# Down projection of the experts and output projection of the attention with the weights stationary, the sums of two batches turned back

## The chip, the core and the metric

The kernel runs on one core of one Trainium2 chip. The metric is the device time of one execution in microseconds, as the median of several runs. One execution is also taken with the hardware profiler; its rows are used below.

## The reference, cut to what matters

There are 16 batches of 100 tokens with 256 features (x), and for each batch 361 context rows of 256 features with a mask. All is float32. Four blocks follow each other, each added to x:

```python
x = x + xattn0(layernorm(x), ctx)       # 16 heads of 64; query i sees the keys j with j % 100 == i
x = x + experts(layernorm(x))           # 8 experts of 192, the best 2 of a token, and a shared one of 192
x = x + xattn1(layernorm(x), ctx, mask) # tanh scores over the context, two scalars per token
x = x + bitlinear_ffn(layernorm(x))     # 256 -> 1024 -> 256, quantised
```

The two products that the change touches are the last ones of the first two blocks:

```python
out = attention_sums.reshape(b, n_q, 1024) @ Wout + bout          # 1024 -> 256
out = sum over experts and shared of  (silu(x @ Wg) * (x @ Wu) * weight) @ Wd   # 9 * 192 = 1728 -> 256
```

## The kernel before

The program first counts the masks and ranks the batches by the number of context rows that count. If every batch fits a table of capacities (`CAPS`, 96 down to 32 rows), which the given inputs do, it takes the path `batches(True, "f")`, and in it `staggered`. The other path (`attend`, `experts`, `score`) is compiled and not run.

`staggered` treats the batches in 8 pairs g. In stage t it weaves three streams: `attention(t + 2)`, `middle(t + 1)` (the experts, `experts_pair`, and the preparation of the scores, `prepare_pair`) and `last(t)` (`score_few` for the two batches, and beside it the feed-forward of the batch before). `weave` runs the streams, which are generators, by turns: it always advances the one with the smallest quotient of steps done and declared steps; declared are 47, 33 and 26. The instructions are emitted in this order, and a scheduler in the framework then sets their order on each engine by its own estimate; on the chip each engine takes its instructions in that fixed order. A pair starts its attention in stage t = g - 2, so stage t = -2 has an attention alone, t = -1 has no scores, t = 6 has no attention, and t = 7 has only scores and feed-forward.

**Attention of a pair** (`attend_pair`). The normalised tokens of both batches are turned (`turned_pair`, tile `xT`, 128 features by 2 x 100 tokens), and GpSimd adds the bias `bout` to x (line 640). Queries are made 128 of the 1024 columns at a time with the weights stationary and the 200 tokens of both batches moving (line 664). `project` (line 650) makes keys and later values of one batch the same way, 361 context rows moving; VectorE multiplies them by the queries (`prT`), TensorE sums over a head into the bank `psim`, and the softmax (`p`) goes through DRAM (`dp`) to be spread over partitions as `pb`. Then, batch by batch, VectorE multiplies the values by `pb` (line 725) and adds up over keys into `accT`, 128 partitions by 4 by 100. At the end of each batch the output projection runs:

```python
po = bank(f"po_{g}_{i}")
for c in range(NH):                       # NH = 8
    nc.tensor.matmul(po[:S, :D], lhsT=accs[c // 4][:, c % 4, :], rhs=wout[:, c, :], ...)
nc.vector.tensor_tensor(xs[i], po[:S, :D], xs[i], ALU.add)
```

So the 100 tokens are stationary and the 256 columns of Wout move; the sum comes out with tokens on partitions and is added to x by VectorE.

**Experts of a pair** (`experts_pair`). The nine experts' 1728 inner columns are 14 chunks of 128. `gated` makes two chunks of gate and up (banks `pgT`, `puT`, line 810) with weights stationary and 200 tokens moving; ScalarE's tanh and VectorE make `hT` of them, `weighted` multiplies by the routing weights, which come back from DRAM (`dw`, `wb`), and `lowered` (line 838) adds the chunk's part of the down projection to the bank `pd` (100 tokens by 2 batches by 256), which a product of zeros has cleared (line 846). There too the tokens of one batch are stationary and the 256 columns of Wd move. At the end VectorE adds `pd` to x (line 874).

**Preparation and scores.** `prepare_pair` transposes the context (bank `pcn`, tile `cn`), picks the rows that count (`pcc`), and makes the projections `tpp` and `fpp`. `score_few` lets VectorE add them (`hf`, line 990), ScalarE take the tanh (line 997) and TensorE sum (`rho`, line 976).

**Feed-forward.** `feed_forward` works in bfloat16 on integers: tokens turned (`pxi`, `xiT`), two halves of gate and up (`pfg`, `pfu`), a quantised `hi`, its turn (`phi`, `hiT`), and the down product `pfd`.

Every float32 product shows as two rows in the profile, each with its own load of the stationary side (PEld); a float32 transpose shows as one.

## Time and profile before

| | |
|---|---|
| median of 3 runs | 1182.46 us (1181.66 to 1182.7) |
| profiled execution | 1183.23 us, its span 1181.5 us |
| granted TensorE clock, mean | 0.938 |
| pd rows (line 838) | 448, 109.1 us busy |
| po rows (line 738) | 256, 59.8 us busy |
| pgT and puT rows (line 810) | 448 and 448, 89.3 and 87.9 us busy |
| transposes pcn (line 905) | 96 |

A row of the profile gives a line, an engine, an operation and the tiles out<-in; a stationary side of 128 rows and 100 columns is written 128*100. PE is TensorE, PEld its weight loads, DVE VectorE, ACT ScalarE, POOL GpSimd, SP the engine that issues most transfers. The span runs from the first to the last instruction. Rows of TensorE overlap each other, so the time that one takes in a dense stretch is read from the starts and not from its duration.

### The profile page before, as it was taken

The numbers are of one execution on the slowest core, as the hardware profiler recorded it, in microseconds if no ns is written. First come the engines' busy times: TensorE is split into PE (matmuls) and PEld (weight loads), VectorE is DVE, ScalarE is ACT, GpSimd is POOL, SyncE is SP. The second block draws the span as 40 slices with busy tenths as digits, with TensorE's granted clock in tenths as the row PEclk, the third lists the DMA queues.
The fourth block names the chain that finished last, engine by engine and source line by source line (L and its number), as shares of the span: only waits on it lengthen the run. The fifth ranks groups of instructions, "written<-read, shape, count | busy, mean of one in ns | idle before, by whom it ended". The sixth has DMA issues, their size and how long they took to land.

```text
span 1181.5 us, 15014 instructions
## 1 busy us (share of the span) xinstructions
PE 1044.0 (88%) x5558; PEld 678.5 (57%) x5558; DVE 843.4 (71%) x1999; ACT 355.6 (30%) x509; POOL 130.1 (11%) x244
## 2 busy tenths in 40 slices
PE   4969989899888999899997999899999999889553
PEld 4536757465455655657555665566656675567432
DVE  2356476758877788777888668777787768787765
ACT  0001102523333334333334223243233323253431
POOL 3010011000320003200130001200031001100100
PEclk9979999999998999999989899999989999989755
DMA  7851033001401013010230104110140103110000
GB/s 233 211 126 52 28 93 83 22 21 29 92 20 35 15 41 80 20 35 15 57 84 0 43 7 95 45 31 20 31 89 4 40 7 82 29 29 18 4 4 11
DMA packets 52463, 58.59 MB, mean 50 GB/s; under 512 B 9129, under 2 KB 51101, under 8 KB 52381
## 3 DMA queue, kind: packets, MB, share of 16 engines
q1 hardware_dynamic: 51564, 54.39, 18.8%
q10 hardware_dynamic: 816, 3.15, 0.7%
q8 instruction: 46, 0.75, 0.3%
q14 instruction: 37, 0.30, 0.1%
HBM read 54.36 MB, written 3.17 MB: 49 GB/s over the span
## 4 chain that ended last, share of the span: by engine, by line
PE 77%; DVE 14%; ACT 4%; POOL 2%; issue 2%; DMA 1%; SPq 0%; ACTq 0%; DVEq 0%; POOLq 0%
PE pkT L650 27%; PE rho L976 9%; PE pd L838 8%; PE pgT L810 7%; PE puT L810 6%; DVE hf L990 4%; PE pqT L664 3%; PE po L738 3%; ACT hf L997 2%; PE psim L692 2%; PE pfd L1118 2%; PE pfg L1081 1%; PE pcc L917 1%; PE pfp L951 1%; PE phi L1110 1%
## 5 line engine op out<-in xcount | busy, mean ns | idle before, releaser
L650 PE MATMUL pkT<-cT_f,wkv 128*128 128x361 f32 x1024 | 371.4, 497 | 17.7 <-DVE pb L725 16.5
L990 DVE TENSOR_TENSOR hf<-tpp,fpp 128x800 f32<-128x800 f32 (+6 forms) x280 | 254.8, 935 | 29.1 <-PE rho L976 15.4
L650 PEld LDWEIGHTS pkT<-cT_f,wkv 128*128 128x128 f32 x1024 | 192.6, 200 | 139.5 <-issue 38.6
L997 ACT ACTIVATE hf<-hf 128x1600 f32<-128x1600 f32 (+5 forms) x140 | 204.6, 1461 | 218.3 <-DVE hf L990 186.4
L976 PE MATMUL rho<-hf,win 128*32 128x480 f32 (+7 forms) x1280 | 141.1, 477 | 36.1 <-ACT hf L997 35.6
L682 DVE TENSOR_TENSOR prT<-pkT,qT 128x300 f32<-128x300 f32 x128 | 59.8, 467 | 75.3 <-PE pkT L650 66.3
L838 PE MATMUL pd<-wd,hT 128*100 128x256 f32 x448 | 109.1, 384 | 0.0
L838 PEld LDWEIGHTS pd<-wd,hT 128*100 128x100 f32 x448 | 72.0, 166 | 38.7 <-issue 14.1
L810 PE MATMUL pgT<-xT_e,wg 128*128 128x200 f32 x448 | 89.3, 341 | 0.0
L725 DVE TENSOR_TENSOR pb<-pkT,pb 128x361 f32<-128x361 f32 x128 | 64.7, 527 | 33.8 <-PE pkT L650 26.6
L810 PE MATMUL puT<-xT_e,wu 128*128 128x200 f32 x448 | 87.9, 338 | 0.0
L976 PEld LDWEIGHTS rho<-hf,win 128*32 128x32 f32 x1280 | 31.8, 114 | 97.1 <-ACT hf L997 52.3
L810 PEld LDWEIGHTS pgT<-xT_e,wg 128*128 128x128 f32 x448 | 77.2, 189 | 15.0 <-issue 5.6
L810 PEld LDWEIGHTS puT<-xT_e,wu 128*128 128x128 f32 x448 | 76.1, 189 | 4.8 <-issue 3.1
L822 ACT ACTIVATE hT<-pgT 128x400 f32<-128x400 f32 (+1 forms) x64 | 29.4, 460 | 141.6 <-PE pgT L810 134.2
L823 DVE SCALAR_TENSOR_TENSOR hT<-hT,pgT 128x400 f32<-128x400 f32 (+1 forms) x64 | 32.9, 514 | 52.3 <-ACT hT L822 51.6
L738 PE MATMUL po<-wout,accT 128*100 128x256 f32 x256 | 59.8, 381 | 0.0
L664 PE MATMUL pqT<-xT_a,wq 128*128 128x200 f32 x256 | 53.0, 355 | 1.9 <-ACT xT_a L634 1.9
L664 PEld LDWEIGHTS pqT<-xT_a,wq 128*128 128x128 f32 x256 | 44.8, 199 | 14.4 <-issue 9.0
L894 POOL TENSOR_SCALAR at<-iota,place 128x96 f32<-128x96 f32 (+15 forms) x48 | 42.2, 898 | 85.8 <-PE pcc L917 83.6
L738 PEld LDWEIGHTS po<-wout,accT 128*100 128x100 f32 x256 | 42.1, 169 | 12.5 <-issue 0.9
L898 POOL TENSOR_SCALAR negf<-iota,cnts 128x96 f32<-128x96 f32 (+7 forms) x16 | 11.9, 741 | 336.4 <-DVE sf L1004 336.1
(221 smaller groups left out, 1127.0 us busy)
## 6 DMA issues: line engine op xcount, KB each, us to landing
pb<-dp SPq DMA_DIRECT2D x64, 361.0 KB
wb<-dw SPq DMA_DIRECT2D x32, 200.0 KB
cT_f<-in_ctxT_dram SPq DMA_DIRECT2D x16, 361.0 KB
wb<-dw SPq DMA_DIRECT2D x32, 100.0 KB
wkv<-in_L_xattn_Wkv_dram ACTq DMA_DIRECT2D x2, 1024.0 KB
x_f<-in_x_dram SPq DMA_DIRECT2D x16, 100.0 KB
out_dram<-x_f SPq DMA_DIRECT2D x16, 100.0 KB
dp<-p SPq DMA_DIRECT2D x8, 180.5 KB
```

The costliest lines, as they stand in the source:

```text
L650: nc.tensor.matmul(ps[:, :T], lhsT=wkv[:, k, at : at + P], rhs=cTs[i][:, k, :], start=k == 0, stop=k == NK - 1,)
L664: nc.tensor.matmul(ps[:, i * 2 * S : (i + 1) * 2 * S], lhsT=wq[:, k, (c + i) * P : (c + i + 1) * P], rhs=xT[:, k, :, :].rearrange("p b s - ...
L682: nc.vector.tensor_tensor(pr[:, :BACK].rearrange("p (c s) -> p c s", s=S), kp[:, :BACK].rearrange("p (c s) -> p c s", s=S), q.unsqueeze(1) ...
L725: nc.vector.tensor_tensor(pb[:, j, :], vp[:, :T], pb[:, j, :], ALU.mult)
L738: nc.tensor.matmul(po[:S, :D], lhsT=accs[c // 4][:, c % 4, :], rhs=wout[:, c, :], start=c == 0, stop=c == NH - 1,)
L810: nc.tensor.matmul(ps[: rows[c], c * 2 * S : (c + 1) * 2 * S], lhsT=w[:, k, (c0 + c) * P : (c0 + c) * P + rows[c]], rhs=xT[:, k, :, :].rea ...
L823: nc.vector.scalar_tensor_tensor(h_, h_, 1.0, pg_, ALU.add, ALU.mult)
L838: nc.tensor.matmul(pd[:, i, :], lhsT=h[: rows[c], at : at + S], rhs=wd[: rows[c], c0 + c, :], start=False, stop=c0 + c == NFC - 1 and i == 1,)
L894: nc.gpsimd.tensor_scalar(at[:rows, c, :], iota[:rows, :cap], place[:rows, c, b : b + 1], None, ALU.is_equal)
L976: nc.tensor.matmul(rho[32 * j : 32 * j + 32, : FM * cap], lhsT=win[:, k, 31 - r : 63 - r], rhs=h2[:, n * cap : (n + FM) * cap], start=r == ...
L990: nc.vector.tensor_tensor(h[:, f : f + n // 2, :], tp[:, k, :].unsqueeze(1).to_broadcast([P, n // 2, cap]), fp[:, k, r * nb + f : r * nb + ...
L997: nc.scalar.activation(h2, h2, AF.Tanh)
```

## The change

The two projections change sides. In `lowered`, 128 of the 256 columns of Wd are stationary and the 200 tokens of both batches move; `pd` holds 128 output features by two halves by 200. In `attend_pair` the same is done with Wout; for this the values of both batches are finished first (the loop over groups of four chunks is now outside, the one over batches inside), and one `po` of both batches comes at the end. A new function, `turned_back`, copies such a bank to SBUF with ScalarE (`dT`; for the attention with the bias added there, in two activations), and, one step later, lets TensorE transpose it in four pieces into a bank `pback`, which VectorE adds to x.

With the bias on partitions, `bout` is loaded as 128 by 2 single elements, GpSimd's adds go, and the path that is not run loads its own row. Room in SBUF is made by sharing: `p` takes a buffer of `prT`, `hiT` one of `hT2`, and `cn` holds one half of the features at a time, so that the picking of the first half precedes the transposes of the second. The declared steps become 45, 34 and 26, and the next pair is loaded at the attention's step 36 in place of 38. The streams have 47, 34 and 26 steps.

```diff
     wr, wr_src = weight("wr", ins["L0_ffn_W_gate_router"], E)
     wt, wt_src = weight("wt", ins["L1_xattn_Ws"], D)
     wf, wf_src = weight("wf", ins["L1_xattn_W"], D)
-    bout = const.tile([S, D], FP, tag="bout", name="bout")
+    bout = const.tile([P, NK], FP, tag="bout", name="bout")
     ebias = const.tile([S, E], FP, tag="ebias", name="ebias")
     wg = const.tile([P, NK, EF], FP, tag="wg", name="wg")
     wu = const.tile([P, NK, EF], FP, tag="wu", name="wu")
...
 
     def load_others():
         load = nc.sync.dma_start
-        load(out=bout, in_=ins["L0_xattn_bout"].to_broadcast([S, D]))
+        with nc.allow_non_contiguous_dma(reason="a few columns"):
+            load(out=bout, in_=ins["L0_xattn_bout"].rearrange("o (k p) -> p (o k)", p=P))
         load(out=ebias, in_=ins["L0_ffn_expert_bias"].to_broadcast([S, E]))
         load(out=wout, in_=wout_src)
         load(out=wr, in_=wr_src)
...
 
     def attend(b, x, cT):
         xn = layernorm(x, f"a{b}")
-        nc.gpsimd.tensor_tensor(x, x, bout, ALU.add)
+        brow = work.tile([S, D], FP, tag="brow", name=f"brow_{b}", bufs=1)
+        nc.sync.dma_start(out=brow, in_=ins["L0_xattn_bout"].to_broadcast([S, D]))
+        nc.gpsimd.tensor_tensor(x, x, brow, ALU.add)
         yield
         xT = transposed(xn, f"a{b}")
         yield
...
         nc.scalar.copy(xT.rearrange("p k b s -> p (k b s)"), ps[:, : NK * 2 * S])
         return xT
 
+    def turned_back(ps, name, bias=None):
+
+        dT = work.tile([P, NK, 2, S], FP, tag="dT", name=f"dT_{name}", bufs=1)
+        if bias is None:
+            nc.scalar.copy(dT.rearrange("p k b s -> p (k b s)"), ps[:, : NK * 2 * S])
+        else:
+            for k in range(NK):
+                nc.scalar.activation(
+                    dT[:, k, :, :].rearrange("p b s -> p (b s)"), ps[:, k * 2 * S : (k + 1) * 2 * S],
+                    AF.Identity, bias=bias[:, k : k + 1],
+                )
+        yield
+        back = bank(f"pback_{name}").rearrange("p (b d) -> p b d", b=2)
+        for i in range(2):
+            for k in range(NK):
+                nc.tensor.transpose(back[:S, i, k * P : (k + 1) * P], dT[:, k, i, :], ident)
+        return back[:S]
+
     def attend_pair(g, xs, cTs):
         xns = normal_pair(xs, f"a{g}")
-        for x in xs:
-            nc.gpsimd.tensor_tensor(x, x, bout, ALU.add)
         yield
         yield
         xT = turned_pair(xns, f"a{g}")
...
                         psim[32 * j : 32 * j + 32, :T], lhsT=heads[:, at : at + 32], rhs=pr,
                         start=i == 0 and c0 == 0, stop=i == 1 and c0 > 0,
                     )
-        p = work.tile([P, NC_, S], FP, tag="p", name=f"p_{g}", bufs=1)
+        p = work.tile([P, NC_, S], FP, tag="prT", name=f"p_{g}", bufs=4)
         p2 = p.rearrange("p c s -> p (c s)")
         nc.gpsimd.memset(p2[:, T:], NEG)
         nc.scalar.copy(p2[:, :T], psim[:, :T])
...
         rows = dp.rearrange("(j r) t -> r j t", r=32)
         for _ in range(4):
             yield
-        for i in range(2):
-            accs = []
-            for c0 in range(0, NH, 4):
+        accs = []
+        for c0 in range(0, NH, 4):
+            acc = work.tile([P, 4, 2, S], FP, tag="accT", name=f"accT_{g}_{c0}")
+            for i in range(2):
                 pb = work.tile([P, 4, T], FP, tag="pb", name=f"pb_{g}_{i}_{c0}", bufs=2)
                 for e in range(2):
                     row = 4 * i + 2 * (c0 // 4) + e
...
                     vp = project(i, c0 + j, 1)
                     nc.vector.tensor_tensor(pb[:, j, :], vp[:, :T], pb[:, j, :], ALU.mult)
                     yield
-                acc = work.tile([P, 4, S], FP, tag="accT", name=f"accT_{g}_{i}_{c0}")
-                nc.vector.tensor_tensor(acc, pb[:, :, :S], pb[:, :, S : 2 * S], ALU.add)
+                own = acc[:, :, i, :]
+                nc.vector.tensor_tensor(own, pb[:, :, :S], pb[:, :, S : 2 * S], ALU.add)
                 for c in range(2, NC_):
                     nc.vector.tensor_tensor(
-                        acc[:, :, : KEYS[c]], acc[:, :, : KEYS[c]],
+                        own[:, :, : KEYS[c]], own[:, :, : KEYS[c]],
                         pb[:, :, c * S : c * S + KEYS[c]], ALU.add,
                     )
-                accs.append(acc)
-            yield
-            po = bank(f"po_{g}_{i}")
+            accs.append(acc)
+        yield
+        yield
+        po = bank(f"po_{g}")
+        for o in range(NK):
             for c in range(NH):
                 nc.tensor.matmul(
-                    po[:S, :D], lhsT=accs[c // 4][:, c % 4, :], rhs=wout[:, c, :],
+                    po[:, o * 2 * S : (o + 1) * 2 * S], lhsT=wout[:, c, o * P : (o + 1) * P],
+                    rhs=accs[c // 4][:, c % 4, :, :].rearrange("p b s -> p (b s)"),
                     start=c == 0, stop=c == NH - 1,
                 )
-            nc.vector.tensor_tensor(xs[i], po[:S, :D], xs[i], ALU.add)
-            yield
+        back = yield from turned_back(po, f"a{g}", bout)
+        for i in range(2):
+            nc.vector.tensor_tensor(xs[i], back[:, i, :], xs[i], ALU.add)
+        yield
 
     def experts_pair(g, xs):
         xns = normal_pair(xs, f"e{g}")
...
 
         def lowered(c0, h, rows):
             for c in range(2):
-                for i in range(2):
-                    at = (2 * c + i) * S
+                for o in range(NK):
                     nc.tensor.matmul(
-                        pd[:, i, :], lhsT=h[: rows[c], at : at + S], rhs=wd[: rows[c], c0 + c, :],
-                        start=False, stop=c0 + c == NFC - 1 and i == 1,
-                    )
-
-        yield
-        pd = psum_rho.tile([S, 2, D], FP, tag="down", name=f"pd_{g}")
+                        pd[:, o * 2 * S : (o + 1) * 2 * S],
+                        lhsT=wd[: rows[c], c0 + c, o * P : (o + 1) * P],
+                        rhs=h[: rows[c], c * 2 * S : (c + 1) * 2 * S],
+                        start=False, stop=c0 + c == NFC - 1 and o == NK - 1,
+                    )
+
+        yield
+        pd = psum_rho.tile([P, NK * 2 * S], FP, tag="down", name=f"pd_{g}")
 
         nc.tensor.matmul(
-            pd.rearrange("p b d -> p (b d)"), lhsT=zero.to_broadcast([1, S]),
-            rhs=zero.to_broadcast([1, 2 * D]), start=True, stop=False,
+            pd, lhsT=zero.to_broadcast([1, P]), rhs=zero.to_broadcast([1, NK * 2 * S]),
+            start=True, stop=False,
         )
         hs = {}
         for c0 in range(0, NFC + 4, 2):
...
             if 0 <= c0 - 4 < NFC:
                 lowered(c0 - 4, *hs.pop(c0 - 4))
             yield
+        back = yield from turned_back(pd, f"e{g}")
         for i in range(2):
-            nc.vector.tensor_tensor(xs[i], pd[:, i, :], xs[i], ALU.add)
+            nc.vector.tensor_tensor(xs[i], back[:, i, :], xs[i], ALU.add)
         yield
 
 
...
             nc.gpsimd.tensor_scalar(neg, iota[:, :cap], cnts[:, b : b + 1], -1e30, ALU.is_ge, ALU.mult)
             negs.append(neg)
 
-            cn = work.tile([P, NK, len(TC), P], FP, tag="cn", name=f"cn_{b}", bufs=1)
-            for k in range(NK):
+            for k in range(NK):
+                cn = work.tile([P, len(TC), P], FP, tag="cn", name=f"cn_{b}_{k}", bufs=1)
                 ps = bank(f"pcn_{b}_{k}")
                 for c, rows in enumerate(TC):
                     nc.tensor.transpose(
...
                     )
                 whole = T // P
                 nc.scalar.copy(
-                    cn[:, k, :whole, :].rearrange("p c d -> p (c d)"), ps[:, : whole * P]
-                )
-                nc.scalar.copy(cn[: TC[-1], k, whole, :], ps[: TC[-1], whole * P : (whole + 1) * P])
+                    cn[:, :whole, :].rearrange("p c d -> p (c d)"), ps[:, : whole * P]
+                )
+                nc.scalar.copy(cn[: TC[-1], whole, :], ps[: TC[-1], whole * P : (whole + 1) * P])
                 yield
-            for k in range(NK):
                 for c, rows in enumerate(TC):
                     to = (2 * k + i) * cap
                     nc.tensor.matmul(
-                        pcc[:, to : to + cap], lhsT=cn[:rows, k, c, :],
+                        pcc[:, to : to + cap], lhsT=cn[:rows, c, :],
                         rhs=at[:rows, c, :], start=c == 0, stop=c == len(TC) - 1,
                     )
             yield
...
             nc.tensor.transpose(
                 ps[:, c * S : (c + 1) * S], hi[:, c * P : (c + 1) * P], ident_bf[:S, :S]
             )
-        hiT = work.tile([P, HID // P, S], BF, tag="hiT", name=f"hiT_{b}", bufs=1)
+        hiT = work.tile([P, HID // P, S], BF, tag="hT2", name=f"hiT_{b}", bufs=4)
         nc.scalar.copy(hiT.rearrange("p c s -> p (c s)"), ps[:, : HID // P * S])
         yield
         ps = bank(f"pfd_{b}")
...
         def attention(g):
             xs, cTs, _ = zip(loaded.pop(2 * g), loaded.pop(2 * g + 1))
             for i, _ in enumerate(attend_pair(g, xs, cTs)):
-                if i == 38 and g + 1 < G:
+                if i == 36 and g + 1 < G:
                     load_pair(g + 1)
                 yield
             attended[g] = xs, cTs
...
         for t in range(-2, G):
             streams = []
             if t + 2 < G:
-                streams.append((47, attention(t + 2)))
+                streams.append((45, attention(t + 2)))
             if 0 <= t + 1 < G:
-                streams.append((33, middle(t + 1)))
+                streams.append((34, middle(t + 1)))
             if t >= 0:
                 streams.append((26, last(t)))
             if t == -1:
```

## The prediction

> **What bounds the kernel now.** I read the page first, then the busy time of the engines in the stretches between the starts of successive attention stages, then TensorE's timeline for the spacing of its rows, and last the three engines around one place where a stage ends and the next begins.
>
> The page: TensorE is busy 88% of the span and carries 77% of the chain that ended last; pkT, pd and po are among its largest lines.
>
> ```profile
> span 1181.5 us, 15014 instructions
> PE 1044.0 (88%) x5558; PEld 678.5 (57%) x5558; DVE 843.4 (71%) x1999; ACT 355.6 (30%) x509; POOL 130.1 (11%) x244
> PE 77%; DVE 14%; ACT 4%; POOL 2%; issue 2%; DMA 1%; SPq 0%; ACTq 0%; DVEq 0%; POOLq 0%
> ```
>
> By stage (columns: stretch, length, PE, PEld, DVE, ACT, POOL busy with counts, granted clock, DMA share, GB/s), a full stage has TensorE at 131.4 of 141 us and VectorE at 110.1. So a saving on TensorE counts, but only some 10 us of idle TensorE and 31 us of idle VectorE stand between the two limits. The last stretch, 87.5 us of the last pair's scores, has neither pd nor po and stays.
>
> ```profile
> 494.00:635.00 141.00, 131.37 (x698) 82.06 (x694) 110.11 (x251) 50.35 (x67) 17.53 (x28) 0.96 0.17 40
> 1094.00:1181.50 87.50, 43.42 (x324) 29.01 (x324) 57.16 (x156) 26.49 (x43) 4.99 (x13) 0.63 0.02 6
> ```
>
> TensorE's timeline (start, us, operation) shows what a row costs when rows stand back to back: take the difference of starts. pgT and puT are already 128 stationary columns with 200 moving; pd is 100 stationary with 256 moving.
>
> ```profile
> 1058.08 1.52 PE L810 MATMUL pgT<-xT_e,wg 128*128 128x200 f32 x8
> 1059.43 1.52 PE L810 MATMUL puT<-xT_e,wu 128*128 128x200 f32 x8
> 1060.79 0.50 PE L810 MATMUL pgT<-xT_e,wg 128*128 128x200 f32 x2
> 1061.13 1.89 PE L838 MATMUL pd<-wd,hT 128*100 128x256 f32 x8
> 1062.85 1.18 PE L810 MATMUL pgT<-xT_e,wg 128*128 128x200 f32 x6
> ```
>
> Eight pgT take 1059.43 - 1058.08 = 1.35 us, 169 ns each; eight pd take 1062.85 - 1061.13 = 1.72 us, 215 ns each.
>
> **The change, part by part.** The number of rows stays (448 for pd, 256 for po: two output halves in place of two batches), the moving side falls from 256 to 200 columns, so a row falls from 215 to 169 ns, 46 ns. pd: 448 x 46 = 20.6 us. po: 256 x 46 = 11.8 us. Both stand in full stages where TensorE is packed.
>
> The Trainium skill, page "TensorE: Matmul & The Clock Gate", section "LDWEIGHTS (loading the stationary operand)", speaks against this: a load takes its columns / 1.2 ns, whatever the rows. By that the 28 more columns cost 23 ns a row (an estimate from the page), 16 us in all if nothing hides them, and the change would end some 9 us slower. The trace has longer loads for the wider shape too (194 against 166 ns mean), but pgT with just that load is spaced at 169 ns, so the load is hidden, and I charge none of it.
>
> Added are 16 turns back of 4 transposes each, 64 rows of 128 moving columns. The nearest row is pcn, three transposes of 128x128 from 592.33 to 592.75, where rho starts: 0.42 / 3 = 140 ns. The lower end is pxT_f, four with 100 moving columns from 617.16 to 617.60, 110 ns. I take 140: 64 x 0.14 = 9.0 us (7.0 at the low end).
>
> The same page, section "Part 4: PE-mode transpose", gives about 275 ns for a transpose inside a kernel; by it the 64 would take 17.6 us (an estimate) and the change would come out 1.6 us slower than before. The trace's own 140 ns decides.
>
> TensorE work thus falls by 20.6 + 11.8 - 9.0 = 23.4 us, of which a full stage has 2.6 + 1.5 - 1.1 = 2.9 us.
>
> What it costs in waits. *The attention's turn* is the expensive one. Before, the first batch's po lay in mid-stage and only the second one's 16 rows ended the stage. Now all 32 rows stand at the end, the attention stream has 47 steps but is woven as 45, so its last steps run after the others have finished, and between po and the next stage come a ScalarE copy, four transposes and two adds. This is the same place before, TensorE, VectorE, ScalarE:
>
> ```profile
> 628.88 3.62 PE L738 MATMUL po<-wout,accT 128*100 128x256 f32 x16
> 632.34 0.34 PE L632 MATMUL pxT_a<-ident,xn_a 100*128 100x100 f32 x2
> 636.83 0.39 PE L632 MATMUL pxT_e<-ident,xn_e 100*128 100x100 f32 x2 [0.36 <-DVE xn_e L332]
> ```
>
> ```profile
> 629.54 3.36 DVE L990 TENSOR_TENSOR hf<-tpp,fpp 128x720 f32<-128x720 f32 x4 [0.45 <-ACT fpp L956]
> 632.83 0.41 DVE L742 TENSOR_TENSOR x_f<-po,x_f 100x256 f32<-100x256 f32 x1
> ```
>
> ```profile
> 629.08 0.74 ACT L956 ACTIVATE fpp<-pfp,cols 128x200 f32<-128x200 f32 x2 [1.89 <-PE pfp L951]
> 631.36 1.40 ACT L997 ACTIVATE hf<-hf 128x1440 f32<-128x1440 f32 x1 [1.53 <-DVE hf L990]
> 633.00 1.41 ACT L997 ACTIVATE hf<-hf 128x1440 f32<-128x1440 f32 x1 [0.23 <-DVE hf L990]
> ```
>
> After: 32 po rows of 169 ns from 628.88 end at 634.3. In the changed program's instruction order dT's two activations are queued on ScalarE behind both tanh (end 634.41); priced by fpp's pair they take 0.74, to 635.15. Transposes 0.56 and rho rows between them: VectorE's first add starts near 635.9, not 632.83. VectorE has finished its four hf at 632.9 and waits 3.0 us, with the next hf queued behind the add. Then two adds (0.41), two statistics (0.43), GpSimd's two steps (0.23 + 0.57) and xn_e (0.41) put the first pxT_e at about 639.2. TensorE has run out by 637.3 and waits 1.9 us; the rest of the queue (pqT, prt, rho) then brings pgT to about 646, 3.5 us after its old 642.49. Of these 3.5, the 16 po rows moved here (5.4 - 3.5 = 1.9) and the transposes (0.6) are in the sum already, so 1.0 us is new idle; VectorE had waits on GpSimd in that stretch of before and makes up the rest. Bounds 0 (rho and pqT cover it) and 3.0 (VectorE's stall passes through whole). I take 1.5, nearest to the 1.0 with some of VectorE's lateness left: 6 x 1.5. The first two boundaries have no scores to cover a turn: copy 0.74, transposes 0.56 and a second batch's normalisation behind them, 2.5 each. Sum 9.0 + 5.0 = 14.0 us.
>
> *The experts' turn*: the order puts six or more pkT rows, rho and the next stage's pieces between the last pd and the transposes, and a rho that needs a later tanh ahead of them; nothing waits on dT (0.49 us on ScalarE, by xT's row). Before, VectorE's add there waited for pd anyway (1.24 us at 581.1). Taken as 0, at most 0.5 each. The last pair's turn falls into 4.94 us in which TensorE waits for wbtf.
>
> *Ends of stages paced by VectorE*: phi waits 2.45 us for hi at 606.07. A TensorE that comes earlier waits longer where VectorE is dense. I charge 0.4 us for 6 stages, 2.4 us; the upper end is the whole 2.9 of a stage.
>
> *Answers of nothing*: 16 GpSimd adds of bout go (16 x 0.723 = 11.6 us of an engine busy 11%). bout's load in 4-byte pieces ranks with the cols loads on SP, issued in 0.37 to 0.47 us, and is first needed near 81 us. The SP order of dp, pb and context loads keeps its shape: the loads for the next pair still go just ahead of the last pb. cn, half as large, makes ScalarE's copy for k = 1 wait for pcc of k = 0, which now precedes pcn of k = 1 on TensorE. p in prT's buffers and hiT in hT2's take buffers whose readers are already past in TensorE's order; at worst a short wait on ScalarE, which is busy 30%.
>
> Sum: 23.4 - 14.0 - 2.4 = 7.0 us. Against the profiled execution, 1183.23 us (span 1181.5, 1.7 around it), 1176.2; the median of the runs, 1182.46, lies 0.8 lower, so 1175.5. About 0.2% (2.4 us) is what a measurement can tell from no change.
>
> **Rivals.** *The turns are covered* (0.20): rho, pxT_a and pqT fill the boundary, the 14.0 and 2.4 vanish: 1182.5 - 23.4 = 1159. For it: TensorE had gaps of only 0.3 us there. Against: the pxT_e order above.
>
> *VectorE keeps the pace* (0.10): each stage's 2.9 us return at phi and pwb: about 1182.
>
> *The boundary opens and the clock falls* (0.29, slower). After a stretch with TensorE half busy, the trace shows the granted clock near half:
>
> ```profile
> 646.00:652.00 6.00, 3.10 (x20) 0.57 (x16) 4.96 (x14) 3.98 (x3) 0.00 (x0) 0.81 0.00 0
> 652.00:657.00 5.00, 5.00 (x13) 2.91 (x12) 0.62 (x3) 0.54 (x2) 0.00 (x0) 0.55 0.15 47
> ```
>
> There eight pkT take 4.6 us (652.14 to 656.77) against 2.6 (584.23 to 586.86): 2.0 us. If VectorE's 3.0 us pass through and one such stretch follows, a boundary costs 5.0: 6 x 5.0 + 5.0 + 2.4 - 23.4 = +14.0, 1196.5. It decides from (23.4 - 2.4 - 5.0) / 6 = 2.7 us a boundary on. For it: 634 to 639 would hold some 2.6 us of TensorE work in 5. Against: TensorE before that is packed with po.
>
> **How the numbers follow.** Forecast 0.41 at 1175.5, own range 1168 to 1180; covered 0.20; paced 0.10; opened 0.29, from 1185 to 1200. Faster 0.41 + 0.20 = 0.61, same 0.10, slower 0.29. The range 1158 to 1195 leaves out under 0.1 on each side.
>
> **What would show it.** Right: pd and po rows at 169 ns, pback four in 0.56, VectorE idle about 3 us ahead of the pback adds, TensorE idle 1 to 2 us before pxT_e, experts' transposes without a wait. Wrong: po or pd spaced above 190 ns, a clock under 0.9 behind the boundary, or phi waiting over 4 us.

## The result and the profile after

The changed kernel takes **1200.4 us** (median of 4 runs, 1195.72 to 1202.33) against 1182.58 of the kernel before beside it (1181.66 to 1183.04). The ratio is 1.0146, 95% interval 1.0115 to 1.0176: 18 us slower, where 7 us less were forecast. The profiled execution took 1201.14 us with a span of 1199.3; before had 1181.5.

The page of the changed kernel, the lines that answer to those shown of before:

```profile
span 1199.3 us, 15155 instructions
PE 1051.0 (88%) x5622; PEld 714.2 (60%) x5622; DVE 842.4 (70%) x1999; ACT 363.2 (30%) x533; POOL 119.9 (10%) x228
PE 71%; DVE 16%; POOL 4%; ACT 4%; issue 2%; DMA 2%; SPq 0%; DVEq 0%; ACTq 0%; POOLq 0%
```

TensorE's busy time rose by 7 us although its rows became shorter, and it lost 6 points of the chain, of which VectorE and GpSimd took over 2 each (ScalarE stayed at 4%): the path now runs through them more often.

By stage (the same columns as before: length, busy times, granted clock): the stage that answers to 494 to 635, and the stretch from the start of the last eight pd rows to the end.

```profile
501.60:645.50 143.90, 131.61 (x701) 87.45 (x700) 109.01 (x249) 51.44 (x70) 17.09 (x26) 0.94 0.17 39
1101.70:1199.30 97.60, 52.38 (x337) 36.53 (x336) 59.99 (x163) 27.85 (x46) 5.00 (x13) 0.57 0.02 6
```

The stage is 2.9 us longer with TensorE as busy as before at a lower clock. The last stretch is 97.6 us at a clock of 0.57; counted from the same row, before has 90.2 at 0.64.

TensorE's timeline (start, us, operation) gives the new spacing:

```profile
1072.29 1.52 PE L835 MATMUL puT<-xT_e,wu 128*128 128x200 f32 x8
1073.98 1.52 PE L862 MATMUL pd<-hT,wd 128*128 128x200 f32 x8
1075.34 1.18 PE L835 MATMUL pgT<-xT_e,wg 128*128 128x200 f32 x6
```

Eight pd rows take 1075.34 - 1073.98 = 1.36 us, 170 ns each, as forecast; the wider load of the stationary side stays hidden. The section "LDWEIGHTS (loading the stationary operand)" of the Trainium skill's page "TensorE: Matmul & The Clock Gate" puts a load at its columns / 1.2 ns. For this shape that isn't a cost on top of the row: loads of 189 ns mean in the trace do not show in the spacing.

The boundary between two stages, on TensorE, VectorE and ScalarE:

```profile
768.40 7.02 PE L760 MATMUL po<-accT,wout 128*128 128x200 f32 x32
775.36 0.72 PE L1002 MATMUL rho<-hf,win 128*32 128x320 f32 x2
776.01 0.32 PE L655 MATMUL pback_a<-ident,dT_a 128*100 128x128 f32 x1
781.40 0.42 PE L635 MATMUL pxT_e<-ident,xn_e 100*128 100x100 f32 x2 [2.90 <-DVE mv_e L328]
```

```profile
769.11 3.03 DVE L1016 TENSOR_TENSOR hf<-tpp,fpp 128x640 f32<-128x640 f32 x4 [0.73 <-ACT fpp L982]
777.13 0.82 DVE L1016 TENSOR_TENSOR hf<-tpp,fpp 128x640 f32<-128x640 f32 x1 [4.99 <-PE rho L1002]
777.87 0.75 DVE L767 TENSOR_TENSOR x_f<-pback_a,x_f 100x256 f32<-100x256 f32 x2
```

```profile
772.23 1.27 ACT L1023 ACTIVATE hf<-hf 128x1280 f32<-128x1280 f32 x1 [0.20 <-DVE hf L1016]
775.46 0.75 ACT L647 ACTIVATE dT_a<-po,bout 128x200 f32<-128x200 f32 x2 [1.96 <-PE po L760]
```

VectorE makes two hf buffers in four instructions and then waits 4.99 us. It waits there not for the turned sums but for a buffer: `hpool` has two, the third hf needs the eight rho rows that free the first, and these stand on TensorE behind all 32 po rows, six of them also behind the first transpose (776.01), which waits for dT. ScalarE is done with both tanh at 773.5 and waits for po. Part of the po rows run at half clock (32 in 7.0 us, against 5.4 at 169 ns). Then come the turn, the adds, two statistics and GpSimd's steps, and TensorE waits 2.90 us for pxT_e. Over the whole kernel (view of waits: sum, times, longest):

```profile
PE pxT_e L635 <- DVE mv_e L328: 14.5, 7, 3.1
PE pxT_e L635 <- DVE xn_e L333: 5.5, 4, 2.9
DVE hf L1016 <- PE rho L1002: 33.3, 28, 5.0
```

Before, TensorE waited 3.8 us for pxT_e in all and VectorE 15.4 for rho.

### The profile page after: what moved, and what is told of

It is laid out like the page before. It is cut to its first block, busy times and chain, and to the rows that moved or that the text cites. A ratio compares the mean times of both kernels' runs of the same rounds, so it can differ in the third digit from the quotient of the medians.

```text
span 1199.3 us, 15155 instructions
## 1 busy us (share of the span) xinstructions
PE 1051.0 (88%) x5622; PEld 714.2 (60%) x5622; DVE 842.4 (70%) x1999; ACT 363.2 (30%) x533; POOL 119.9 (10%) x228
## 4 chain that ended last, share of the span: by engine, by line
PE 71%; DVE 16%; POOL 4%; ACT 4%; issue 2%; DMA 2%; SPq 0%; DVEq 0%; ACTq 0%; POOLq 0%
PE pkT L669 21%; PE rho L1002 8%; PE pgT L835 7%; PE puT L835 6%; PE pd L862 6%; PE pqT L683 5%; PE po L760 4%; DVE hf L1016 3%; PE psim L711 3%; ACT hf L1023 2%; PE pfd L1144 2%; PE pfp L977 2%; DVE pb L745 2%; DMA pb<-dp 2%; PE pfg L1107 1%
## 5 line engine op out<-in xcount | busy, mean ns | idle before, releaser
L669 PE MATMUL pkT<-cT_f,wkv 128*128 128x361 f32 x1024 | 362.5, 485 | 11.4 <-DVE pb L745 10.7
L669 PEld LDWEIGHTS pkT<-cT_f,wkv 128*128 128x128 f32 x1024 | 187.1, 195 | 122.3 <-issue 32.5
L1002 PE MATMUL rho<-hf,win 128*32 128x480 f32 (+7 forms) x1280 | 154.6, 476 | 32.5 <-ACT hf L1023 32.2
L862 PE MATMUL pd<-hT,wd 128*128 128x200 f32 x448 | 89.3, 337 | 0.0
L862 PEld LDWEIGHTS pd<-hT,wd 128*128 128x128 f32 x448 | 76.5, 189 | 18.8 <-issue 9.9
L683 PE MATMUL pqT<-xT_a,wq 128*128 128x200 f32 x256 | 64.6, 403 | 1.9 <-ACT xT_a L637 1.9
L683 PEld LDWEIGHTS pqT<-xT_a,wq 128*128 128x128 f32 x256 | 52.8, 230 | 9.5 <-issue 6.7
L760 PE MATMUL po<-accT,wout 128*128 128x200 f32 x256 | 50.9, 362 | 1.1 <-DVE accT L750 1.1
L760 PEld LDWEIGHTS po<-accT,wout 128*128 128x128 f32 x256 | 50.3, 214 | 1.7 <-DVE accT L750 1.4
L921 POOL TENSOR_SCALAR at<-iota,place 128x96 f32<-128x96 f32 (+15 forms) x48 | 36.2, 772 | 128.2 <-PE pcc L943 119.4
```

The lines of the kernel that those rows point to most:

```text
L669: nc.tensor.matmul(ps[:, :T], lhsT=wkv[:, k, at : at + P], rhs=cTs[i][:, k, :], start=k == 0, stop=k == NK - 1,)
L683: nc.tensor.matmul(ps[:, i * 2 * S : (i + 1) * 2 * S], lhsT=wq[:, k, (c + i) * P : (c + i + 1) * P], rhs=xT[:, k, :, :].rearrange("p b s - ...
L760: nc.tensor.matmul(po[:, o * 2 * S : (o + 1) * 2 * S], lhsT=wout[:, c, o * P : (o + 1) * P], rhs=accs[c // 4][:, c % 4, :, :].rearrange("p ...
L862: nc.tensor.matmul(pd[:, o * 2 * S : (o + 1) * 2 * S], lhsT=wd[: rows[c], c0 + c, o * P : (o + 1) * P], rhs=h[: rows[c], c * 2 * S : (c + ...
L921: nc.gpsimd.tensor_scalar(at[:rows, c, :], iota[:rows, :cap], place[:rows, c, b : b + 1], None, ALU.is_equal)
L1002: nc.tensor.matmul(rho[32 * j : 32 * j + 32, : FM * cap], lhsT=win[:, k, 31 - r : 63 - r], rhs=h2[:, n * cap : (n + FM) * cap], start=r == ...
```

## The experiments

The 25 us between forecast and result had candidates in every step, so the runs take the change apart. In all of them "the body" is the time up to the start of the last eight pd rows, and "the rest" what follows; both come from one profiled execution of each kernel, which can lie some us off the median. The executions of one kernel differ by their mean granted clock: no_turn took 1158.4 us at 0.935 and 1171.9 at 0.924, and its profile, 1158.9, is at 0.935. The table is the base of what follows.

| kernel | median us | ratio to before, 95% | body | rest |
|---|---|---|---|---|
| before | 1182.58 | | 1091.3 | 90.2 |
| after | 1200.40 | 1.0115 to 1.0176 | 1101.7 | 97.6 |
| cn_alone | 1185.37 | 1.0015 to 1.0043 | 1087.3 | 96.6 |
| experts_alone | 1197.20 | 1.0109 to 1.0182 | 1097.2 | 96.3 |
| attention_alone | 1203.94 | 1.0147 to 1.0220 | 1107.1 | 97.2 |
| cn_whole | 1189.40 | 1.0045 to 1.0095 | 1091.9 | 96.6 |
| no_turn | 1163.64 | 0.9806 to 0.9913 | 1061.3 | 95.8 |
| no_turn_att | 1166.95 | 0.9855 to 0.9903 | 1073.2 | 91.4 |
| no_turn_exp | 1179.36 | 0.9959 to 0.9991 | 1079.7 | 95.9 |
| copy_only | 1180.82 | 0.9973 to 1.0010 | 1083.9 | 95.5 |
| attention_whole | 1196.25 | 1.0102 to 1.0147 | 1102.1 | 90.0 |
| experts_sim | 1182.32 | 0.9974 to 1.0008 | 1085.1 | 96.2 |

**cn_alone**: the kernel before with the context's transpose halved as in the change, nothing else.

```diff
-cn = work.tile([P, NK, len(TC), P], FP, tag="cn", bufs=1)
 for k in range(NK):
+    cn = work.tile([P, len(TC), P], FP, tag="cn", bufs=1)
     ... transposes and copies of k ...
-for k in range(NK):
     ... pcc of k ...
```

> The kernel before with one part of the change alone: cn holds one half of the features at a time. Theory T (two causes): in the last pair's preparation nothing runs beside it, so transposes, ScalarE copies and picking of the halves go one after the other; in the changed kernel that stretch, from the start of the last pair-6 phi to the first rho of the last pair, is 23.2 us (1110.55 to 1133.73) against 16.2 (1099.69 to 1115.93). So 5 to 8 us slower here too, 1187 to 1191. Rival R (the turn and the granted clock make the whole loss, the stretch is longer only because the clock happened to be low there): within 2 us of before.

Measured +3.4 us, between the two. The body became shorter, the rest longer by 6.4 us.

**experts_alone**: the kernel before with the experts' projection and its turn as in the change.

```diff
-pd[:, i, :], lhsT=h[...], rhs=wd[: rows[c], c0 + c, :]
+pd[:, o * 2 * S : (o + 1) * 2 * S], lhsT=wd[..., o * P : (o + 1) * P], rhs=h[...]
+back = yield from turned_back(pd, f"e{g}")
```

> The kernel before with the experts' down projection alone changed: weights stationary, 200 tokens moving, its sum turned back, declared steps 34, hiT in hT2's buffers. Theory T: the saving of pd, 448 rows x 46 ns = 20.6 us less 32 transposes of 140 ns = 4.5 us, is mostly kept: 1166 to 1174. Rival R (a TensorE that is loaded less gets a lower clock, whatever is saved is lost): 1180 or more.

A miss: 1197.2, in the rival's range but not by its cause, for experts_sim below has as low a mean clock (0.929 against 0.930) and is 15 us faster. TensorE waits in front of pback_e, not for ScalarE's copy but for VectorE's pb (view of waits):

```profile
PE pback_e L652 <- DVE pb L743: 10.8, 6, 6.0
PE pback_e L652 <- ACT dT_e L641: 0.6, 1, 0.6
```

pb has nothing to do with the experts. What ties the two is the PSUM bank: `bank` hands out five in turn, and the one that the transposes get still holds a pkT that VectorE has not multiplied. Everything behind the transposes on TensorE waits too.

**attention_alone**: the change without its experts' part (halved cn stays).

```diff
-back = yield from turned_back(pd, f"e{g}")
-pd[:, o * 2 * S : (o + 1) * 2 * S], lhsT=wd[..., o * P : (o + 1) * P], rhs=h[...]
+pd[:, i, :], lhsT=h[...], rhs=wd[: rows[c], c0 + c, :]
```

> The changed kernel with the experts' down projection as before: the attention's part with its block of 32 po rows at the end of a stage, its turn, and the halved cn. Theory T: all of the loss is here, and the saving of pd is missing: above 1205. Rival R: between before and after, 1185 to 1200.

1203.9, between the two ranges, and as slow as the whole change. So neither part pays by itself, and they don't add up: experts_alone costs 15 us, attention_alone 22, both together 18.

**cn_whole**: the change with the whole cn kept; dT takes qT's buffers for want of space.

```diff
-dT = work.tile([P, NK, 2, S], FP, tag="dT", bufs=1)
+dT = work.tile([P, NK, 2, S], FP, tag="qT", bufs=3)
```

> The changed kernel with cn whole again (both halves of the features at once, dT in qT's buffers to make the room). Theory T: the last preparation is short again, 5 to 8 us off: 1192 to 1196. Rival R: as the changed kernel, 1198 to 1202.

1189.4, faster than the theory's range: the halved cn, which the prediction charged nothing for, costs 11 us here, 9.8 of them in the body. The theory's place for it, the last preparation, is wrong: from the last phi to the first rho of the last pair the changed kernel takes 23.2 us (1110.55 to 1133.73) and cn_whole still 22.4 (1100.73 to 1123.17). The same 5622 rows keep TensorE busy 1051.0 us in the changed kernel and 1043.8 here, and the mean granted clock is lower, 0.921 to 0.925 in its four executions against 0.927 to 0.930 in the five of cn_whole. Rows that the halving doesn't touch take longer: po 50.9 against 48.3 us, pfp 19.9 against 18.0, pqT 64.6 against 62.1, pkT 362.5 against 360.2. A clock lower by 0.007 over 1190 us is up to 8 us, so most of the cost seems to come by way of the clock; how the halving brings it down is not shown. dT's other buffers don't explain it: in both kernels dT waits for nothing but po and pd. By itself the halving cost the kernel before 3.4 us.

**before_again**: the kernel before, unchanged, to see whether the rest's 90.2 us are its own or one execution's.

> The kernel before, once more, for the granted clock of its last stretch. In the first profile the last 88 us have 64 us at half clock; in all four kernels tried so far that stretch is 95 us with 78 to 83 us at half clock, though cn_whole and experts_alone have the same instructions there. If the place of the clock's windows against the program decides (theory T), another execution of before shows 95 us too, with less half clock elsewhere, and 1182 all the same. If the changed kernels really differ there (rival R), it shows 88 us again.

1183.05, and a rest of 90.2 again, as the rival says: it goes with the program.

**no_turn**: cn_whole without the turns; VectorE adds po and pd as they lie.

```diff
-back = yield from turned_back(po, f"a{g}", bout)
+yield
-nc.vector.tensor_tensor(xs[i], back[:, i, :], xs[i], ALU.add)
+nc.vector.tensor_tensor(xs[i], po[:S, i * 100 : i * 100 + D], xs[i], ALU.add)
```

> cn_whole without the turns: no ScalarE copy, no transposes, VectorE adds parts of the banks pd and po to x as they are, so that the output projections' results are put in wrong places. Rows of 200 columns and the order of steps stay. Theory T (the turn at the stage's boundary takes back what the shorter rows bring): 704 x 46 ns = 32 us less, of which VectorE's pace may take a part: 1152 to 1168. Rival R (VectorE paces the stages, shorter rows bring nothing whatever the turn): 1175 or more.

1163.6, within the theory's range. In the body of these profiles the shorter rows bring 1091.3 - 1061.3 = 30.0 us; the two turns cost 1189.4 - 1163.6 = 25.8 us in the medians and 30.6 in the body.

**attention_first**: cn_whole with the attention declared as 54 steps for 45, so that po has other work beside it.

```diff
-streams.append((45, attention(t + 2)))
+streams.append((54, attention(t + 2)))
```

> cn_whole with the attention's declared steps 54 in place of 45: its last steps come at 47/54 of a stage, so the po block and the turn lie among the other streams' work. Theory T (the turn costs because nothing covers it): 5 to 15 us under cn_whole's 1189.4, unless the start of the next stage, which po covered before, opens instead. Rival R (the rows and the clock cost it, wherever the turn stands): 1187 to 1192.

A miss: 1199.96, worse by 10.6 us. The wait for pxT_e is gone, but po no longer fills the end of the stage, and TensorE waits there for the scores instead:

```profile
PE pwb L1057 <- ACT wbtf L1054: 34.4, 7, 5.2
```

In cn_whole that wait was 18.9 us. The mean granted clock fell too, from 0.930 to 0.916.

**po_split**: cn_whole with po in two halves of 16 rows, the first in mid-stage, in psim's bank.

```diff
-po = bank(f"po_{g}")
+po = psum_rho.tile([P, 512], FP, tag="sim", name=f"po_{g}")[:, : NK * 2 * S]
+... cleared by a product of zeros; after each c0: for c in range(c0, c0 + 4), for o: matmul
-streams.append((45, attention(t + 2)))
+streams.append((47, attention(t + 2)))
```

> cn_whole with po in two parts: the 16 rows of the first four chunks as soon as their sums are there, in mid-stage, into the bank psim has left, and only 16 rows at the stage's end; declared steps 47 of 48. Theory T: in the changed kernel the first rho of a stage stands behind 32 po rows, VectorE's third hf has no buffer until it has run (5.0 us idle at 777.1); 16 rows fewer (2.7 us) at 6 boundaries are worth 10 to 16 us: 1173 to 1180. Rival R (only the turn's own chain, copy to xn_e, counts): 1186 to 1190.

A miss: 1202.4 (1.0163). With the order shifted, pback_e again meets a held bank:

```profile
PE pback_e L655 <- DVE pb L744: 12.3, 6, 5.4
PE po L763 <- DVE accT L749: 14.9, 6, 2.9
```

**experts_sim**: experts_alone, but the turned sums lie in psim's bank, which is free there.

```diff
-back = bank(f"pback_{name}")
+back = psum_rho.tile([P, 512], FP, tag="sim", name=f"pback_{name}")
```

> The experts' projection alone changed, as in experts_alone (1197.2 us), but the sums that are turned back lie in the PSUM bank of the attention's scores (psim), which is free at that point, and not in one of the five rotating banks. Theory: in experts_alone the four transposes wait 11.4 us in sum because the rotating bank they get still holds a pkT that VectorE's pb has not taken, and the slow clock follows these waits; without that wait pback_e has under 1.5 us of idle time ahead of it, and the kernel runs at 1180 to 1188. Rival: VectorE is late there anyway, the bank only shows it, and the next row that needs a bank waits as long: 1193 to 1199.

1182.3: the bank alone cost 14.9 us. The wait for pb is gone:

```profile
PE pback_e L652 <- ACT dT_e L641: 0.6, 1, 0.6
```

The experts' half of the change then equals the kernel before: 6.2 us less body, 6.0 more rest.

**attention_whole**: cn_whole with the experts' projection as before; it completes the square.

```diff
-dT = work.tile([P, NK, 2, S], FP, tag="dT", bufs=1)
+dT = work.tile([P, NK, 2, S], FP, tag="qT", bufs=3)
 ... attention_alone, with cn and its two loops over k as in the kernel before
```

> The attention's projection and its turn alone changed, with whole cn (dT in qT's buffers); the experts' projection as before. It completes the square before 1182, experts_alone 1197, cn_whole 1189. Theory: the attention's part is what opens the boundary, and halved cn costs it what it costs the changed kernel, about 11 us: 1203.9 - 11 = 1190 to 1196, so that the attention's part costs some 10 us by itself and the experts' part next to it brings 3 to 5. Rival: the parts add up (experts +15, so the attention's part must bring 7): 1173 to 1178.

1196.3, just above the theory's range: the attention's half costs 14 us by itself.

**copy_only**: cn_whole with ScalarE's copy kept and the transposes left out.

```diff
-back = bank(...); four nc.tensor.transpose(back[...], dT[:, k, i, :], ident)
-return back[:S]
+return dT.rearrange("p k b s -> p (k b s)")[:S]
```

> The changed kernel with whole cn (cn_whole, 1189.4 us), keeping ScalarE's copy of the sums but leaving the 64 transposes out: VectorE adds the copy as it lies, so that tokens and columns stand in the wrong places. Without copy and transposes it ran at 1163.6 (no_turn), so the turns cost 25.8 us. Theory: the waits of the boundary hang on the copy and on the rows' work about equally: 64 transposes of 140 ns are 9 us, and with them goes their place behind rho; 1172 to 1180. Rival A: the transposes' place in TensorE's order is nearly all of it, and the copy is hidden: 1162 to 1168. Rival B: the copy's wait is nearly all of it: 1183 to 1189.

1180.8, just above the theory's range: without the 64 transposes 8.6 us are saved. That 64 x 0.14 = 9.0 lies so near is chance, for other things moved as well: TensorE's waits for pxT_e rose from 20.3 to 27.9 us, and the mean granted clock fell from 0.930 to 0.922. So the run doesn't part the turn's cost into transposes and copy; it shows that a copy without transposes still costs 17.2 us.

**no_turn_att** and **no_turn_exp**: cn_whole without the one turn or the other, by no_turn's edit.

> The changed kernel with whole cn (cn_whole, 1189.4 us) without the attention's turn: VectorE adds po as it lies (tokens and columns in the wrong places, the bias bout missing); the experts' turn stays. Without either turn it ran at 1163.6, so the two cost 25.8 us. Theory: nearly all of it is the attention's turn, because there the next stage hangs on the turned sum, as the prediction's split has it (18.5 to 4.5): 1166 to 1172. Rival: both cost alike, by their transposes and by what they do to the order: 1175 to 1178.

> The same with the experts' turn left out instead: VectorE adds pd as it lies, the attention's turn stays. Theory: only the 32 transposes of 140 ns and some waits go: 1182 to 1186. Rival: both turns cost alike: 1175 to 1178.

1166.95, in the theory's range, and 1179.36, between the two ranges. The attention's turn costs 22.5 us, 18.7 of them in the body (the rest is 5.2 us longer with it than without); the experts' costs 10.0 (12.2 in the body). 18.7 + 12.2 = 30.9 fits the 30.6 of both together, so in these profiles the two terms add up; by the medians 22.5 + 10.0 = 32.5 stands against 25.8.

**fill_pwb** and **fill_before**: 12 products of no use, 24 rows, ahead of the pwb after the last pd, in experts_sim and in the kernel before.

```diff
 ps = bank(f"pwb_{b}")
+if b == B - 3:
+    for _ in range(12):
+        nc.tensor.matmul(ps[:, 16 : 16 + 2 * S], lhsT=wout[:, 0, :P], rhs=wout[:, 1, : 2 * S], start=True, stop=True)
```

> experts_sim (1182.3 us) with 12 products of zero use (24 rows of 128 stationary columns and 200 moving, about 4.1 us) ahead of the pwb of batch 13, into unused columns of its bank: there TensorE otherwise waits 0.6 and 4.5 us after the last pd. Nothing else changes. In experts_sim the granted clock falls to half at 1089.3, in that wait, and stays there for 30.7 us, though TensorE is busy 95% from 1095 to 1110; before has 6.8 us of it at that place. Theory: the wait sets the clock of the stretch that follows; with it filled, the stretch from the last pd to the end falls from 94.8 to 86 to 90 us and the kernel runs at 1174 to 1178, below the kernel before. Rival: the clock falls anyway a few us later, at the waits for hi and for the context's copies, and nothing is won: 1181 to 1185.

> The kernel before (1182.3 us) with the same 24 rows at the same place: the control for fill_pwb. Theory: here the clock came back after 6.8 us, so filling the wait saves at most those 6.8 us at half clock, of which TensorE was busy some 3: 1179 to 1182. Rival: the rows delay pwb, or move the stretch against the clock's windows, and the clock then stays low for 30 us as in the other kernels: 1184 to 1190.

In the profiled execution of fill_pwb (1183.47 us, the slowest of its ten) the theory falls. The rows fill the wait, and the clock falls some 7 us later and stays low for 24 us; the rest is 95.8 us against 96.2 in experts_sim. The control has 89.4 against 90.2 in the kernel before. The medians, 1180.28 (ratio 0.9958 to 0.9997), just under the rival's range, and 1181.22 (0.9967 to 1.0002), in the theory's, are not told apart from one another. But four of the ten executions of fill_pwb and two of the ten of fill_before took 1175.7 to 1176.6 us, at a mean granted clock of 0.938 to 0.949, where none of the 19 of the kernel before beside them was under 1180.0 or over 0.942. So the filled wait may bring the higher clock more often; whether it does stays open, for no profile caught one of these. fill_pwb is the fastest version that leaves nothing out, by some 0.2%, about what can just be measured.

## Why the prediction was wrong

Counted in the body, its steps can be held one by one against the runs (all in us; plus is slower):

| step of the sum | forecast | measured in the profiles | by |
|---|---|---|---|
| shorter pd and po rows, less VectorE's pace | -30.0 | -30.0 | before and no_turn |
| attention's turn (14.0 and 32 transposes) | +18.5 | +18.7 | no_turn_att and cn_whole |
| experts' turn (0 and 32 transposes) | +4.5 | +12.2 | no_turn_exp and cn_whole |
| halved cn | 0 | +9.8 | cn_whole and after |
| the last stretch, which "stays" | 0 | +7.4 | before and after |

The forecast column sums to -7.0, the measured one to +18.1; the spans differ by +17.8. The measured figures are good to a few us, not to tenths: by the medians less the rest the first four are -24, +17, +9 and +10, and the first po row, ahead of which nothing is turned, already starts at 88.6 us in no_turn_att and at 90.6 in cn_whole.

**Right: the spacing of the rows.** A row takes 169 ns, 46 less. That the column then says 30.0 to the tenth is luck: by the medians it is 24, no_turn also holds the small edits that were charged nothing (bout's load, the GpSimd adds, the shared buffers), and larger terms cancel in it. From before to no_turn TensorE's waits for pxT_e rise from 3.8 to 19.5 us, its waits for phi fall from 33.0 to 23.9, and the pkT rows, which the change leaves alone, go from 371.4 to 357.0 us of busy time. So the 2.4 us, charged for longer waits at phi, were not found there.

**Right: a transpose at 140 ns.** Four take 0.53 us in the changed kernel (timeline), where 0.56 were forecast:

```profile
728.36 0.60 PE L655 MATMUL pback_e<-ident,dT_e 128*100 128x128 f32 x4
728.89 0.81 PE L1002 MATMUL rho<-hf,win 128*32 128x360 f32 x8
```

The about 275 ns that the Trainium skill's page "TensorE: Matmul & The Clock Gate", section "Part 4: PE-mode transpose", gives for a bf16 transpose appear in the profile as the duration of one float32 pback_e (median 273 ns), but the durations of successive transposes overlap; what they cost the kernel is nearer the spacing.

**Right in size, not in mechanism: the attention's turn.** 18.5 was forecast, 18.7 is the body's cost, which by the above is luck in its tenths. The prediction had VectorE idle for 3 us ahead of the pback adds because dT is behind two tanh on ScalarE, and TensorE then idle for pxT_e. On the chip the tanh are done in time, and VectorE is idle for 5 us ahead of the third hf, because the rho rows that free its buffer are behind 32 po rows and a transpose. The prediction listed what is queued behind the waiting instruction on VectorE and ScalarE, but not what is queued behind the moved po rows on TensorE. no_turn_att has the same po rows and no turn of the attention's; its waits are (view of waits):

```profile
DVE hf L1017 <- PE rho L1003: 15.4, 23, 2.1
PE pxT_e L635 <- DVE xn_e L333: 10.5, 9, 3.0
PE pxT_e L635 <- DVE mv_e L328: 8.4, 5, 1.8
```

In cn_whole VectorE's waits for rho are 32.7 us, so these go with the turn. TensorE's for pxT_e are 20.3 there and 18.9 here: they come with the rest of the change, which puts all 32 po rows at the stage's end, and not with the turn that the prediction charged them to. And the forecast's 14.0 us were to be waits, but from no_turn_att to cn_whole TensorE's idle time grows by only 3.4 us and its busy time by 20.5 (1023.3 to 1043.8). The 32 transposes have 6.2 of these; the rest are rows that both kernels have, at a mean granted clock of 0.930 against 0.937.

**Failed: "the experts' turn ... taken as 0, at most 0.5 each".** It is 12.2 - 4.5 = 7.7 us, nearly 1 us each, in the profiles, and some 5 us, 0.6 each, by the medians. The reason given, that nothing waits on dT, is right in the changed kernel: pback_e has only 0.6 us of idle time ahead of it. So the cost isn't a wait at the turn. Between no_turn_exp and cn_whole TensorE's busy time for lines that the turn doesn't touch grows: pfp from 15.5 to 18.0 us, po from 45.9 to 48.3, rho from 152.6 to 155.3, pkT from 357.5 to 360.2, 10.3 in sum, without one row more. For pfp it is the clock: its median row takes 417 ns against 333. pfp and po stand at the end of a stage, so the turn seems to shift more of these ends into half clock; which of its instructions does so wasn't tried. In another order it costs more: experts_alone and po_split pay 11 to 12 us in waits for a PSUM bank that a pkT holds, and experts_sim shows for the first of them that this is the bank's doing. Banks in rotation were no step of the prediction, although a turn takes one more of them.

**Failed: cn "charged nothing".** The prediction saw that pcn of k = 1 would stand behind pcc of k = 0, and let it pass. There are 8 pairs; 9.8 us is 1.2 us for each, and most of it seems to be the lower clock (cn_whole), not the place of pcn behind pcc.

**Failed: "the last stretch ... stays".** Its work did stay, but for the last turn's four transposes. What changed is the granted clock. Either part brings it alone, the halved cn (cn_alone, 96.6 us) and the experts' projection (experts_sim, 96.2), and together they bring little more (97.6). Of 7 us some 13 us behind the last pd rows' start, before and experts_sim (windows view):

```profile
1104.00:1111.00 7.00, 6.54 (x55) 6.26 (x55) 2.32 (x10) 2.27 (x8) 1.25 (x4) 1.00 0.06 17
```

```profile
1098.00:1105.00 7.00, 6.92 (x36) 6.79 (x34) 2.15 (x10) 2.15 (x8) 1.46 (x4) 0.50 0.05 15
```

In before the clock is back at 1.00 there; in experts_sim it is 0.50 and 36 rows take as long as 55. Of the kernels in the table only before and attention_whole, which have the old pd rows and the whole cn, and, in part, no_turn_att have the short rest (po_split, not in the table, has 91.4). Why the clock comes back in these and not in the others stays open: in fill_pwb's profile the wait ahead of pwb is filled and the clock stays low all the same, so that wait alone doesn't decide it. Nor is it fixed for a kernel: one execution of the kernel before took 1175.9 us at a mean clock of 0.944 (its others 0.934 to 0.942), one of experts_sim 1174.4 at 0.939 (0.929 to 0.934). Which stretch of them had the higher clock isn't known, for no profile caught such a one.

**The rivals.** "The boundary opens and the clock falls" had the right side and, at 1196.5, the nearest time. Its waits and its lower clock did come (20.0 us for pxT_e, a mean clock of 0.923 against 0.938), but not at its price: of the attention's turn (18.7 - 4.5 - 5.0) / 6 = 1.5 us a boundary are left, where it needed 2.7, and the waits for pxT_e stand in no_turn as well, inside the 30 us that were won. What made the change slower are the two terms set to zero and the clock of a stretch thought out of reach. "Covered" is refuted by the 25.8 us that the two turns cost, and "VectorE keeps the pace" by no_turn, where the shorter rows won 19 us in the medians.

## What to carry to other kernels

When a step is moved to a stage's end, list what stands behind it on its own engine, and ask of each whose buffer it frees: here the work behind po freed the buffer that VectorE needed. A detour through a copy and a transpose takes a PSUM bank out of the rotation, and a bank is only free when its last reader is done; where another bank is idle, give it that one (15 us in experts_sim). And a loop that is cut in two to save space (write all, read all, turned into write, read, write, read) is not free: it cost 3.4 us by itself and 11 here, most of it in rows elsewhere.

## What the runs showed of the hardware

The granted clock can stay at half while TensorE has no idle time at all in the records. In fill_pwb (windows view):

```profile
1097.00:1104.00 7.00, 7.00 (x38) 7.00 (x36) 3.15 (x13) 1.95 (x7) 1.93 (x5) 0.50 0.05 15
```

The rows there are pcn transposes, pcc products with 32 moving columns, pfd and pxT_f. The Trainium skill, page "TensorE: Matmul & The Clock Gate", section "Part 1: The HAM clock gate (the "warmup" mystery)", has the full clock come back after one busy window of about 3.4 us. Here 7 us with a matmul or transpose always in flight don't bring it back. The same page says that transposes don't count as busy the way products do, which would fit pcn and pxT_f; but products alone follow (ptp, ptw and pfp, at 1105 to 1111.5 with 0.35 us of idle time), and they still run at half speed: pfp takes 2.98 us for its eight rows, in before 1.57.
